# First-layer results of eight experts: transposed by way of DRAM and VectorE's block transposes instead of TensorE

## Chip, core and metric

The kernel runs on one NeuronCore of a Trainium2 chip. The metric is the device time of one execution in microseconds, as the median of several executions. The engines are TensorE (PE in the profile; its weight loads are PEld), VectorE (DVE), ScalarE (ACT), GpSimd (POOL) and SyncE (SP, which here only issues DMAs). Each works through its own instructions in order and waits on semaphores.

## What is computed

A graph layer over 625 nodes and 20,000 edges is followed by a mixture-of-experts layer over the 625 rows that come out (`x`, 625 x 1024, all in float32). Only the second matters here:

```python
sh = _gelu(jnp.einsum('td,sdh->sth', xf, sW1) + sb1[:, None, :])
shared = (jnp.einsum('sth,shd->std', sh, sW2) + sb2[:, None, :]).mean(axis=0)
gates = xf @ rW + rb
topk_vals, topk_idx = jax.lax.top_k(gates, TOP_K)           # two of eight
h = _gelu(jnp.einsum('td,edh->eth', xf, W1) + b1[:, None, :])
y = jnp.einsum('eth,ehd->etd', h, W2) + b2[:, None, :]
moe = jnp.einsum('te,etd->td', w, y)                         # w: softmax of the two
out = x + shared + moe
```

The model width is 1024, the hidden width 256 (`H`), and there are eight experts and two shared ones.

## The kernel before

The graph layer and the shared experts' first layer come first (to about 156 us). The rows that the router has given to the experts lie in 11 tiles of 128 slots (`NJ` = 11): tiles 4 to 10 are whole (one expert each), tiles 0 to 2 hold two experts of 64 slots, and tile 3 holds four of 32. A matmul of a part writes its own rows of the result, and parts run beside one another.

**First layer, loop at L1542.** The tiles are taken in the order 4, 5, 6, 0, 7, 1, 8, 2, 9, 10, 3 (`tiles`, L1533). In step `s` the code emits, in this order: the second half of the transposes of tile `s-1` (`turn`, L1490, only for tiles whose rows TensorE turns); the gather of tile `s` on GpSimd's queue and its transposition (`fetch`, L1474); the product with W1 of tile `s-1` (`expert_in`, L1508); and the middle of tile `s-2` (`expert_mid`, L1521).

- `fetch`: six tiles (`by_quarters`: 4, 5, 0, 1, 2, 10) are gathered as quarter rows by four indirect DMAs (L1465), so that VectorE's transposes of 32 x 32 blocks (L1482) give the columns that TensorE needs. The other five (6, 7, 8, 9, 3) are turned by TensorE in two halves (L1493, `p_x`); ScalarE copies the first half out of PSUM (L1499), VectorE the second (L1497). `copy_w1` (L1501) has ScalarE copy weights that a second or later part of a tile needs.
- `expert_in`: 16 matmul instructions for a whole tile into `p_h`, then VectorE copies `p_h` (128 slots x 256) to `hj` in SBUF (L1516, two buffers).
- `expert_mid`: TensorE turns the two 128 x 128 halves of `hj` into PSUM (L1524, `p_hT`), and ScalarE applies GELU with the bias and writes `hjT` (L1527), the stationary operand of the second layer.

The middles of the last two tiles (10 and 3) are emitted after the second-layer products of tile 4 (L1570).

**Second layer, loop at L1592.** The tiles are taken in the order 4, 5, 6, 0, 1, 2, 3, 7, 8, 9, 10 (`ORDER`). Each gives two halves of 512 columns (`expert_out`, L1559, `p_yj`); VectorE copies both halves to `ys` for the first four tiles, and later VectorE copies one and ScalarE the other (L1600, L1602); GpSimd scatters the rows to `yt` in DRAM (L1604). Ahead of it ScalarE makes 12 copies of W2 parts (`w2m`, L1590). Then SyncE loads `yt` back by node (L1615), while TensorE makes the shared experts' second layer (`p_o`, L1655, from `sw2` and `shT`), VectorE adds (L1626) and the rows are stored (L1640).

**What sets the order.** The engines' queues are laid out at compile time by a list scheduler that goes by the order of emission, its own estimate of when operands are ready, and the free buffers, so the order in the trace is near that of the code but not the same (the trace has some `p_o` products ahead of the second half of tile 6, for example). `tc.issue_after(x)` puts the instructions of its block behind `x` on their own engine, without a wait. PSUM has eight banks: five called `acc` (`p_x`, `p_yj`, most of `p_o`) and three called `mm` (`p_h`, `p_hT`, the rest of `p_o`).

**SyncE's queue** near the change: the eight 1 MB loads of `w2a` (L1179). The last, `load_w2(NE - 1)` at L1553, can start only when tile 5's product is done, because the turned rows of tiles 4 and 5 lie in that part of `w2a`. Then `sw2` (L1578, 2 MB), which takes memory that the first layer's weights held, and `x1` (L1581, 2.5 MB).

Of the kernel before, what the change touches and what calls it, by code (L numbers as in the profile page):

```python
# [8 lines left out]
F32 = mybir.dt.float32  # L9
# [5 lines left out]
AF = mybir.ActivationFunctionType  # L15
# [8 lines left out]
H = 256  # L24
NE = 8
NS = 2
TP = 125
# [16 lines left out]
NJ = 11  # L44
# [9 lines left out]
HK = H // 128  # L54
# [399 lines left out]
def sparse_kernel(  # L454
# [24 lines left out]
    nc = tc.nc  # L479

    def pool(stack, name, bufs=1, side="left", **kw):
        return stack.enter_context(tc.tile_pool(name=name, bufs=bufs, side=side,
                                                reuse_waits="tile", **kw))
# [5 lines left out]
    dram = ctx.enter_context(tc.tile_pool(name="dram", bufs=1, space=bass.MemoryType.DRAM))  # L489
    h2d = dram.tile([N, D], F32, name="h2d")  # L490
    x1d = dram.tile([N, D], F32, name="x1d")

    yt = dram.tile([2 * YB, D], F32, name="yt")

# [3 lines left out]
    def ps_mm(name):  # L498
        return psum[0].tile([128, 512], F32, tag="mm", name=name, bufs=3)
# [68 lines left out]
    ident = const.tile([128, 128], F32, name="ident")  # L568
# [210 lines left out]
    def first_row():  # L779
        x0 = xh[:TP, 0, :]  # L780
        h = rows.tile([TP, D], F32, tag="h", name="h_0")
        part = fbig.tile([TP, 3], F32, name="part")
        with tc.issue_after(behind.ins):
            nc.vector.tensor_reduce(part[:, 0:1], x0[:, :HALF], axis=AX.X, op=ALU.add)
        with tc.issue_after(table.ins):
            nc.scalar.activation(h[:, HALF:], x0[:, HALF:], AF.Identity, accum_out=part[:, 1:2])
        last = nc.vector.tensor_scalar(part[:, 2:3], part[:, 0:1], part[:, 1:2], -1.0 / D, op0=ALU.add, op1=ALU.mult)
        moved = nc.scalar.activation(h[:, :384], x0[:, :384], AF.Identity, bias=part[:, 2:3])
        with tc.issue_after(last.ins):
            last = nc.vector.tensor_scalar(h[:, 384:], x0[:, 384:], part[:, 2:3], None, op0=ALU.add)  # L790
        hs[0] = h
        return last, moved
# [264 lines left out]
    last, moved = first_row()  # L1057
# [120 lines left out]
    def load_w2(e):  # L1178
        nc.sync.dma_start(w2a[:, e], W2[e].rearrange("(k p) d -> p k d", p=128))  # L1179
# [261 lines left out]
    mid = pool(ctx, "mid")  # L1441
    hjT = mid.tile([128, NJ, HK, 128], F32, name="hjT")
    xts = ExitStack()
    xt = pool(xts, "xt", 2, side="right")
# [5 lines left out]
    def parts(j):  # L1450
        if j < NH2:
            return (0, HS, e_of[j]), (HS, 128, e_of[NH2 + j])
        if j < NM2:
            return [(QS * i, QS * (i + 1), e_of[nt + i]) for i in range(4)]
        return ((0, 128, e_of[NH2 + j - 1]),)

    xsT, p_hs, w1m = {}, {}, {}
    acts = []

    rows = {}  # L1460
# [1 line left out]
    def gather(j):  # L1462
        if j in by_quarters:
            for a in range(4):
                nc.gpsimd.indirect_dma_start(  # L1465
                    out=rows[j][:, a * (D // 4) : (a + 1) * (D // 4)], out_offset=None,
                    in_=h2d.rearrange("n (b f) -> (n b) f", b=4),
                    in_offset=bass.IndirectOffsetOnAxis(ap=tok4[:, a, j : j + 1], axis=0))
        else:
            nc.gpsimd.indirect_dma_start(  # L1470
                out=rows[j], out_offset=None, in_=h2d,
                in_offset=bass.IndirectOffsetOnAxis(ap=tok[:, j : j + 1], axis=0))

    def fetch(j):  # L1474
        if j in tiles[:2]:
            t_ = w2a[:, NE - 1, tiles.index(j)].rearrange("p (k n) -> p k n", k=KD)
        else:
            t_ = xt.tile([128, KD, 128], F32, tag="xsT", name=f"xsT_{j}")
        xsT[j] = t_
        if j in by_quarters:  # L1480
            with tc.issue_after(turned[-1].ins):
                nc.vector.transpose(t_.rearrange("p k (a r) -> p a k r", a=4), rows[j].rearrange("p (a c k) -> p a k c", a=4, k=KD))  # L1482
        else:
            half_row[j] = rows[j]
            turn(j, 0)
        copy_w1(j)
# [3 lines left out]
    def turn(j, g):  # L1490
        p = ps_acc(f"p_x{g}_{j}")
        for k in range(4):
            nc.tensor.transpose(p[:, k * 128 : (k + 1) * 128], half_row[j][:, 4 * g + k :: KD], ident)  # L1493
        o = xsT[j][:, 4 * g : 4 * g + 4, :]
        pv = p.rearrange("p (k n) -> p k n", k=4)
        if g:
            turned.append(nc.vector.tensor_copy(o, pv))  # L1497
        else:
            acts.append(nc.scalar.copy(o, pv))  # L1499
# [8 lines left out]
    def expert_in(j):  # L1508
        p = ps_mm(f"p_h_{j}")
        for k in range(KD):  # L1510
            for a, b, e in parts(j):
                nc.tensor.matmul(p[a:b, :H], xsT[j][:, k, a:b],  # L1512
                                 w1m[j, a][:, 0, k, :] if a else w1a[:, bass.ds(e, 1), k, :],
                                 start=(k == 0), stop=(k == KD - 1))
        h = xt.tile([128, H], F32, tag="hj", name=f"hj_{j}")
        nc.vector.tensor_copy(h, p[:, :H])  # L1516
        p_hs[j] = h

    bT = vT[:, KD + NS * HK :].rearrange("p (e t) -> p e t", t=HK)

    def expert_mid(j):  # L1521
        p = ps_mm(f"p_hT_{j}")
        for t in range(HK):
            nc.tensor.transpose(p[:, t * 128 : (t + 1) * 128], p_hs[j][:, t * 128 : (t + 1) * 128], ident)  # L1524
        for t in range(HK):
            for a, b, e in parts(j):
                done = nc.scalar.activation(hjT[:, j, t, a:b], p[:, t * 128 + a : t * 128 + b], AF.Gelu,  # L1527
                                     bias=bT[:, bass.ds(e, 1), t])
        acts.append(done)

# [2 lines left out]
    tiles = (*whole[:3], 0, whole[3], 1, whole[4], 2, *whole[5:], NH2)  # L1533
# [8 lines left out]
    for s in range(NJ + 2):  # L1542
        if 0 < s <= NJ and tiles[s - 1] in half_row:
            turn(tiles[s - 1], 1)
        if s < NJ:
            if s > 2:
                rows[tiles[s]] = io.tile([128, D], F32, tag="io", name=f"xs_{tiles[s]}")
                gather(tiles[s])
            fetch(tiles[s])
        if 0 <= s - 1 < NJ:  # L1550
            expert_in(tiles[s - 1])
        if s == 2:
            load_w2(NE - 1)  # L1553
        if 0 <= s - 2 < NJ - 2:
            expert_mid(tiles[s - 2])
    ORDER = (*whole[:3], *range(NM2), *whole[3:])
    w2m, p_ys = {}, {}

    def expert_out(j, s):  # L1559
        p_ys[j, s] = p = ps_acc(f"p_yj_{j}_{s}")  # L1560
        for k in range(HK):
            for a, b, e in parts(j):
                made = nc.tensor.matmul(p[a:b], hjT[:, j, k, a:b],  # L1563
                                        (w2m[j, a, k] if a else w2a[:, bass.ds(e, 1), k])[..., s * 512 : (s + 1) * 512],
                                        start=(k == 0), stop=(k == HK - 1))
        return made

    for s in range(2):
        expert_out(ORDER[0], s)
    for j in tiles[-2:]:  # L1570
        expert_mid(j)
    xts.close()
    in_w.close()

    late = pool(ctx, "late", side="right")
    sw2 = late.tile([128, NS, HK, D], F32, name="sw2")
    for i in range(NS):
        nc.sync.dma_start(sw2[:, i], sW2[i].rearrange("(k p) d -> p k d", p=128))  # L1578
    x1 = late.tile([TP, NT, D], F32, name="x1")
    for a, b in ((0, 3), (3, NT)):  # L1580
        nc.sync.dma_start(x1[:, a:b], x1d[a * TP : b * TP].rearrange("(t p) d -> p t d", p=TP))  # L1581
    gat = pool(ctx, "gat", 15, side="right")

    loads, (off,) = nc.values_load_multi_w_load_instructions(flag, min_val=0, max_val=EC * 4 + 1)
# [7 lines left out]
    for n, j in enumerate(ORDER):  # L1592
        y = gat.tile([128, D], F32, tag="y", name=f"ys_{j}")
        for s in range(2):
            at = slice(s * 512, (s + 1) * 512)
            if n:
                made = expert_out(j, s)
            p = p_ys[j, s]
            if s or n < 4:
                nc.vector.tensor_copy(y[:, at], p)  # L1600
            else:
                nc.scalar.copy(y[:, at], p)  # L1602

        sent.append(nc.gpsimd.indirect_dma_start(  # L1604
            out=yt, out_offset=bass.IndirectOffsetOnAxis(ap=row[:, j : j + 1], axis=0), in_=y, in_offset=None,
            bounds_check=2 * YB - 1, oob_is_err=False))
        for s in sent[:-1]:
            tc.declare_no_dep(sent[-1].ins, s.ins, reason="rows of different slots")

    gs = {}  # L1610
    for d in range(NT):
        for a in range(2):
            at = a * YB + 1 + d * TP
# [29 lines left out]
    for d in range(NT):  # L1643
# [3 lines left out]
        for at in ((0, 512), (512, D)) if d < NT - 1 else ((0, 512), (512, 768), (768, D)):  # L1647
            n = at[1] - at[0]
            at = slice(*at)
            p = (ps_mm if banks % 8 > 4 else ps_acc)(f"p_o_{d}_{at.start}")  # L1650
# [59 lines left out]
```

## Time and profile before

| What | us |
|---|---|
| Median of 3 runs (lowest, highest) | 285.66 (285.14, 286.66) |
| Profiled execution, time | 284.5 |
| Profiled execution, span of the trace | 282.6 |
| TensorE busy in the span | 276.2 (98%) |
| VectorE, ScalarE, GpSimd busy | 172.1, 100.4, 64.5 |
| First layer of the experts (first to last `p_h` product) | 156.5 to 202.1 |
| Second layer of the experts (`p_yj`) | 202.1 to 248.3 |
| Shared experts' second layer, from there to the last product | 248.3 to 277.6 |
| 22 transposes of `hj` (L1524), first and last start | 163.9, 205.9 |
| Granted TensorE clock | 1.00 |

The page lists, for each engine, busy time, share of the span and instructions; then the span in 40 slices; the DMA queues; the chain of work that ended last, by engine and line; and groups of instructions with busy time, mean duration in ns, and the idle time ahead of them with what ended it. A line of the timeline has the start and the duration in us, the engine (SPq is the issuing of DMAs on SyncE's queue), the line of the code, the operation, and output <- input. Matmuls overlap in the array, so the time that one takes from TensorE is the distance between starts, not its duration.

### The profile page before, as it was taken

The numbers are of one execution on the slowest core, as the hardware profiler recorded it, in microseconds if no ns is written. First come the engines' busy times: TensorE is split into PE (matmuls) and PEld (weight loads), VectorE is DVE, ScalarE is ACT, GpSimd is POOL, SyncE is SP. The second block draws the span as 40 slices with busy tenths as digits, with TensorE's granted clock in tenths as the row PEclk, the third lists the DMA queues.
The fourth block names the chain that finished last, engine by engine and source line by source line (L and its number), as shares of the span: only waits on it lengthen the run. The fifth ranks groups of instructions, "written<-read, shape, count | busy, mean of one in ns | idle before, by whom it ended". The sixth has DMA issues, their size and how long they took to land.

```text
span 282.6 us, 4458 instructions
## 1 busy us (share of the span) xinstructions
PE 276.2 (98%) x1531; PEld 185.1 (65%) x1531; DVE 172.1 (61%) x435; ACT 100.4 (36%) x232; POOL 64.5 (23%) x128
## 2 busy tenths in 40 slices
PE   8999999999999999999999999999999999999992
PEld 6777777788888555677777887778544324444452
DVE  5899999999875889838911444323330211116892
ACT  3456418334642323354101363564089011100000
POOL 9810110000000023411046655540020222210000
PEclk9999999999999999999999999999999999999999
DMA  7999981000000999995999484440284453339982
GB/s 238 362 334 359 345 288 48 2 0 2 1 0 9 389 371 425 424 415 195 387 410 394 134 271 129 125 147 4 57 335 181 181 216 139 148 135 349 380 306 78
DMA packets 22084, 61.58 MB, mean 218 GB/s; under 512 B 2467, under 2 KB 8294, under 8 KB 21033
## 3 DMA queue, kind: packets, MB, share of 16 engines
q1 hardware_dynamic: 16093, 44.32, 42.3%
q0 software_dynamic: 5680, 16.58, 16.3%
q10 hardware_dynamic: 284, 0.35, 0.4%
q8 instruction: 14, 0.23, 0.4%
q14 instruction: 13, 0.11, 0.1%
HBM read 43.19 MB, written 18.82 MB: 219 GB/s over the span
## 4 chain that ended last, share of the span: by engine, by line
PE 88%; DVE 6%; DMA 3%; SPq 1%; ACT 0%; issue 0%
PE p_pr L955 15%; PE p_h L1512 14%; PE p_yj L1563 14%; PE p_o L1655 12%; PE p_sh L1145 12%; PE p_y L1030 6%; PE p_agg L984 5%; DMA xh<-in_x_dram 3%; DVE st L776 2%; PE cnt L933 2%; PE p_x L1493 2%; PE p_t L843 2%; DVE ohs L902 1%; PE p_hT L1524 1%; PE p_gate L1195 1%; PE p_y L1031 1%
## 5 line engine op out<-in xcount | busy, mean ns | idle before, releaser
L955 PE MATMUL p_pr<-wg,nT 128*125 128x286 f32 x240 | 62.2, 409 | 0.2
L955 PEld LDWEIGHTS p_pr<-wg,nT 128*125 128x125 f32 x240 | 43.3, 187 | 12.5 <-ACT nT L849 1.2
L1563 PE MATMUL p_yj<-w2a,hjT 128*128 (+2 forms) x88 | 38.8, 595 | 0.0
L1655 PE MATMUL p_o<-sw,shT 128*125 128x512 f32 (+1 forms) x88 | 36.1, 553 | 0.0
L1145 PE MATMUL p_sh<-h2T,sw 128*128 128x313 f32 (+1 forms) x128 | 35.3, 429 | 0.0
L1512 PE MATMUL p_h<-w1a,xsT 128*128 (+2 forms) x144 | 32.7, 380 | 0.0
L1600 DVE COPY ys<-p_yj 128x512 f32<-128x512 f32 x15 | 10.4, 691 | 36.0 <-PE p_yj L1563 36.0
L1563 PEld LDWEIGHTS p_yj<-w2a,hjT 128*128 128x128 f32 (+2 forms) x88 | 14.4, 168 | 22.7 <-issue 22.1
L1145 PEld LDWEIGHTS p_sh<-h2T,sw 128*128 128x128 f32 x128 | 23.6, 189 | 8.5 <-issue 0.2
L1655 PEld LDWEIGHTS p_o<-sw,shT 128*125 128x125 f32 x88 | 16.4, 187 | 17.1 <-issue 16.1
L1512 PEld LDWEIGHTS p_h<-w1a,xsT 128*128 128x128 f32 (+2 forms) x144 | 22.8, 163 | 6.5
L1465 POOL DMA_INDIRECT xs<-h2d,tok x24 | 22.7, 946 | 18.5 <-PE p_x L1493 7.6
L1604 POOL DMA_INDIRECT yt<-ys,row x11 | 10.7, 970 | 52.1 <-DVE ys L1600 52.1
L1041 POOL DMA_DIRECT2D x1d<-xh x10 | 5.7, 576 | 71.7 <-DVE flagf L726 62.1
L1516 DVE COPY hj<-p_h 128x256 f32<-128x256 f32 x11 | 4.7, 425 | 25.4 <-PE p_h L1512 25.4
L1030 PE MATMUL p_y<-wo_t,eT 128*125 128x512 f32 (+1 forms) x40 | 18.8, 592 | 0.0
L1527 ACT ACTIVATE hjT<-p_hT,vT 128x128 f32<-128x128 f32 (+2 forms) x34 | 8.6, 335 | 23.9 <-PE p_hT L1524 23.9
L984 PE MATMUL p_agg<-P,CT 125*125 125x288 f32 x100 | 15.5, 305 | 0.0
L1512 PE MATMUL p_h<-w1m,xsT 128*64 128x256 f32 (+1 forms) x96 | 14.7, 381 | 0.0
L1563 PE MATMUL p_yj<-w2m,hjT 128*64 128x512 f32 (+1 forms) x48 | 14.1, 595 | 0.0
L1626 DVE SCALAR_TENSOR_TENSOR x<-g,wab,x 125x1024 f32<-125x1024 f32 (+1 forms) x12 | 13.2, 1105 | 1.4 <-DMA g<-yt 1.2
L903 DVE TENSOR_TENSOR ohs<-ohs,cols 125x1024 f16<-125x1024 f16 (+1 forms) x22 | 14.0, 636 | 0.0
(307 smaller groups left out, 417.6 us busy)
## 6 DMA issues: line engine op xcount, KB each, us to landing
w1a<-in_L_ffn_W_dram SPq DMA_DIRECT2D x8, 1024.0 KB
w2a<-in_L_ffn_W_dram SPq DMA_DIRECT2D x8, 1024.0 KB
yt<-zero SPq DMA_DIRECT2D x2, 2560.0 KB
g<-yt SPq DMA_DIRECT2D x10, 512.0 KB
sw<-in_L_ffn_sW_dram SPq DMA_DIRECT2D x4, 1024.0 KB
x1d<-xh POOLq DMA_DIRECT2D x5, 448.0 KB
h2d<-h POOLq DMA_DIRECT2D x5, 448.0 KB
out_dram<-x SPq DMA_DIRECT2D x4, 448.0 KB
```

What stands on the lines that cost most here:

```text
L903: last = nc.vector.tensor_tensor(os, os, both(VV_, 128)[1], op=ALU.mult)
L955: product = nc.tensor.matmul(p[:TP, :F], nT[:, k, m * TP : (m + 1) * TP], wg[:, k, r, :], start=(k == 0), stop=(k == KD - 1))
L984: nc.tensor.matmul(p[:TP, : F + 2], CT[:, m, at : at + TP], P[:, m, r, i], start=(m == 0 and i == 0), stop=(m == NT - 1 and i == 1))
L1030: nc.tensor.matmul(ps[s][:TP, :], eT[:n, k, :], wo_t[:n, k, at], start=(k == 0), stop=False)
L1145: nc.tensor.matmul(p[:, : z - a], sw1[:, i, k, t * 128 : (t + 1) * 128], h2T[:, k, a:z], start=(k == 0), stop=(k == KD - 1))
L1465: nc.gpsimd.indirect_dma_start(out=rows[j][:, a * (D // 4) : (a + 1) * (D // 4)], out_offset=None, in_=h2d.rearrange("n (b f) -> (n b) f", ...
L1512: nc.tensor.matmul(p[a:b, :H], xsT[j][:, k, a:b], w1m[j, a][:, 0, k, :] if a else w1a[:, bass.ds(e, 1), k, :], start=(k == 0), stop=(k == ...
L1563: made = nc.tensor.matmul(p[a:b], hjT[:, j, k, a:b], (w2m[j, a, k] if a else w2a[:, bass.ds(e, 1), k])[..., s * 512 : (s + 1) * 512], star ...
L1600: nc.vector.tensor_copy(y[:, at], p)
L1604: sent.append(nc.gpsimd.indirect_dma_start(out=yt, out_offset=bass.IndirectOffsetOnAxis(ap=row[:, j : j + 1], axis=0), in_=y, in_offset=No ...
L1626: added.append(nc.vector.scalar_tensor_tensor(*args, op0=ALU.mult, op1=ALU.add))
L1655: nc.tensor.matmul(p[:TP, :n], shT[:, i, k, own], sw2[:, i, k, at], start=(i == 0 and k == 0), stop=False)
```

## The change

The two TensorE transposes of each tile's `hj` go. Instead:

- VectorE's copy writes `hj` with the columns in another order (quarters of 64: for each, 32 of the first 128 columns and 32 of the second), into one buffer instead of two. SyncE stores `hj` to a new DRAM tensor `hd` and then loads it back in four DMAs, one for each group of 32 partitions of `hjT`, so that partition group `q` holds quarter `q` of the columns of all 128 slots.
- VectorE's block transpose of 128 x 256 turns that to `hT`, a new SBUF tile with one buffer, and GELU reads `hT` (SBUF) where it read `p_hT` (PSUM).
- The middle of a tile is emitted one step later (`s-3`), behind the `hj` copy of that step. The last two move into the second-layer loop, behind the copies of its second and third tile.
- `sw2` is issued after the last store of `hj`, the last tile's four loads after `sw2`, and `x1` after `sw2` too.

```diff
+    hd = dram.tile([NJ, 128, H], F32, name="hd")
...
-        h = xt.tile([128, H], F32, tag="hj", name=f"hj_{j}")
-        nc.vector.tensor_copy(h, p[:, :H])
-        p_hs[j] = h
+        h = xt.tile([128, H], F32, tag="hj", bufs=1, name=f"hj_{j}")
+        copied.append(nc.vector.tensor_copy(h.rearrange("p (q c r) -> p c q r", q=4, c=HK),
+                                           p[:, :H].rearrange("p (c q r) -> p c q r", c=HK, q=4)))
+        moved.append(nc.sync.dma_start(hd[j], h))
+        if j != tiles[-1]:
+            to_quarters(j)
+
+    def to_quarters(j):
+        for q in range(4):
+            nc.sync.dma_start(hjT[32 * q : 32 * q + 32, j].rearrange("t c (b r) -> t (c b r)", b=4)
+                              .rearrange("t (b x) -> t b x", b=4),
+                              hd[j].rearrange("(b t) (q x) -> q t b x", b=4, q=4)[q])
...
     def expert_mid(j):
-        p = ps_mm(f"p_hT_{j}")
-        for t in range(HK):
-            nc.tensor.transpose(p[:, t * 128 : (t + 1) * 128], p_hs[j][:, t * 128 : (t + 1) * 128], ident)
+        p = mid.tile([128, HK, 128], F32, tag="hT", name=f"hT_{j}")
+        with tc.issue_after(copied[-1].ins):
+            nc.vector.transpose(p.rearrange("p c (b t) -> p c b t", b=4),
+                                hjT[:, j].rearrange("p c (b r) -> p (c b r)", b=4)
+                                .rearrange("p (b c r) -> p c b r", b=4, c=HK))
...
-                done = nc.scalar.activation(hjT[:, j, t, a:b], p[:, t * 128 + a : t * 128 + b], AF.Gelu,
+                done = nc.scalar.activation(hjT[:, j, t, a:b], p[:, t, a:b], AF.Gelu,
...
-        if 0 <= s - 2 < NJ - 2:
-            expert_mid(tiles[s - 2])
+        if 0 <= s - 3 < NJ - 2:
+            expert_mid(tiles[s - 3])
...
-    for j in tiles[-2:]:
-        expert_mid(j)
...
     for i in range(NS):
-        nc.sync.dma_start(sw2[:, i], sW2[i].rearrange("(k p) d -> p k d", p=128))
+        with tc.issue_after(moved[-1].ins):
+            last = nc.sync.dma_start(sw2[:, i], sW2[i].rearrange("(k p) d -> p k d", p=128))
+    with tc.issue_after(last.ins):
+        to_quarters(tiles[-1])
...
     for a, b in ((0, 3), (3, NT)):
-        nc.sync.dma_start(x1[:, a:b], x1d[a * TP : b * TP].rearrange("(t p) d -> p t d", p=TP))
+        with tc.issue_after(last.ins):
+            nc.sync.dma_start(x1[:, a:b], x1d[a * TP : b * TP].rearrange("(t p) d -> p t d", p=TP))
...
-                nc.vector.tensor_copy(y[:, at], p)
+                copied.append(nc.vector.tensor_copy(y[:, at], p))
...
+        if n in (1, 2):
+            expert_mid(tiles[n - 3])
```

More of the change, by code (lines that the diff above doesn't have):

```diff
@@ L1455, in parts @@
         return ((0, 128, e_of[NH2 + j - 1]),)
-    xsT, p_hs, w1m = {}, {}, {}
+    xsT, w1m, copied, moved = {}, {}, [], []
     acts = []
```

## The prediction, made before the changed kernel was run

> **What bounds the kernel now.** I read the page first: engine shares, then the chain.
>
> ```profile
> PE 276.2 (98%) x1531; PEld 185.1 (65%) x1531; DVE 172.1 (61%) x435; ACT 100.4 (36%) x232; POOL 64.5 (23%) x128
> ...
> PE 88%; DVE 6%; DMA 3%; SPq 1%; ACT 0%; issue 0%
> ...
> L1516 DVE COPY hj<-p_h 128x256 f32<-128x256 f32 x11 | 4.7, 425 | 25.4 <-PE p_h L1512 25.4
> ```
>
> TensorE is busy from end to end, and from the start of the experts (156.5 us) to the last product (277.6) the chain is TensorE alone; VectorE waits for it (25.4 us ahead of the `hj` copies). So time taken off TensorE there is time off the kernel, unless it becomes a wait. Next the timeline at one step of the experts' loop (start, duration, engine):
>
> ```profile
> 184.86 0.36 PEld L1524 LDWEIGHTS p_hT<-ident,hj 128*128 128x128 f32 x2
> 185.08 0.38 PE L1524 MATMUL p_hT<-ident,hj 128*128 128x128 f32 x2
> 185.19 0.52 PEld L1493 LDWEIGHTS p_x<-ident,xs 128*128 128x128 f32 x4
> 185.28 0.42 DVE L1516 COPY hj<-p_h 128x256 f32<-128x256 f32 x1 [0.76 <-PE p_h L1512]
> 185.30 0.49 PE L1493 MATMUL p_x<-ident,xs 128*128 128x128 f32 x3
> ```
>
> Read starts, not durations: the two transposes of `hj` start at 185.08, the next work at 185.30. A pair holds TensorE for 0.22 us. Last, the line of the block transposes, and SyncE's queue (start, time of the issues):
>
> ```profile
> L1482 DVE STREAM_TRANSPOSE xsT<-xs x4: 2031/2046/2056, 165.4 to 191.0; 128x1024 f32<-128x1024 f32 x4
> ```
>
> ```profile
> 0.75 0.39 SPq L531 DMA_DIRECT2D ety_i<-in_edge_type_dram  x1
> 1.20 0.41 SPq L531 DMA_DIRECT2D src_i<-in_src_dram  x1
> 1.65 0.43 SPq L546 DMA_DIRECT2D xh<-in_x_dram  x1
> ```
>
> ```profile
> 132.82 31.64 SPq L1179 DMA_DIRECT2D w2a<-in_L_ffn_W_dram  x8
> 202.19 0.88 SPq L1578 DMA_DIRECT2D sw<-in_L_ffn_sW_dram  x2
> 203.12 4.69 SPq L1581 DMA_DIRECT2D x<-x1d  x2
> ```
>
> SyncE can start a DMA every 0.45 us, and between 164.5 and 202.2 it has nothing to do. The change puts a chain of its own there.
>
> **Removed.** 22 transposes, 11 pairs. Six pairs in the loop cost 0.22; three that follow a half tile cost 0.28 (172.37 to 172.65); the last two together 0.44 (205.61 to 206.05). Sum 1.32 + 0.84 + 0.44 = **2.6 us**, all on the bounding engine. Nothing on TensorE waited for `hj`, so no stall goes with it; the bounds are 2.4 (all at 0.22) and 2.9 (the short gaps after half tiles close too). [...]
>
> **Added on VectorE and ScalarE.** One block transpose of 128x256 for each tile: a quarter of L1482's 2.04 us, so 0.51 (bounds: 0.42, the copy of as many elements, and 2.04). In the fullest step VectorE has the copy 0.43, the transpose 0.51, the copy of `p_x` 0.69 and L1482 2.04, together 3.67 of a step of 4.0: it fits. Behind the new transpose stands the copy of `p_x` (172.49 + 0.43 + 0.51 + 0.69 = 174.12); the product needs it after its first eight matmuls, 173.09 - 0.28 + 1.7 = 174.5. Spare: 0.4 us. That is the thinnest cover in the loop: a late transpose stalls TensorE almost one for one. GELU out of SBUF and the permuted order of the `hj` copy I take at their old price (within 0.1 us either way); TensorE waits for neither inside the loop, since products of the second layer begin after it.
>
> **Added on SyncE and in the queues.** For each tile one store of 128 KB (1 KB rows) and four loads of 32 KB in 256 B pieces. No row shows this pair. The nearest by the trace's records of DMA completions: the output store of 112 rows of 1 KB issued at 277.02 has landed on most of its 16 engines after 1.8 us, on the last after 3.8; that of 117 rows at 278.08 after 1.7 and 2.5; the 78 KB load issued at 0.75 after 1.9, the next after 3.0. I take 1.85 for the store (1.7 to 3.8) and 1.9 for a load (1.6 to 3.0), the typical engine, since the loop moves 43 to 313 GB/s and stragglers are few there. Round trip: 0.1 + 1.85 + 0.1 + three starts of 0.45 + 1.9 = 5.3 us. The block transpose comes two steps after the copy, 8.0 us: hidden, with 2.7 to spare. SyncE, in order, is held by a tile for 0.1 + 1.85 + four starts (1.8) = **3.75 us, of a step of 4.0** (202.24 - 160.20 over ten steps is 4.2, less 0.2). It just keeps up. With one `hj` buffer, the copy of the next tile also waits for the store.
>
> One transfer breaks into this: the last `w2a` load, 1 MB, issued at 164.09 and landed 5.2 us later, in the window 164.5 to 168.7 with a DMA share of 0.89 at 313 GB/s. In the changed kernel SyncE ends tile 4's loads at 160.7 + 1.85 + 0.1 + 1.8 = 164.45, and `w2a` is ready before tile 5's copy ends (164.55): it goes first, and tile 5's store lands behind it in the same rings at 164.45 + 5.2 + 0.2 = 169.85. Its four loads hold SyncE till 171.75, tile 6's store lands at 173.65, and only then may VectorE copy tile 0 (due at 172.05): copy 174.13, transpose 174.64, `p_x` 175.33. TensorE needs `p_x` at 173.09 - 0.72 + 1.7 = 174.07. **Stall 1.3 us**, once; later steps catch up by 0.25 each. Bounds: 0 (the store goes first) and 2.
>
> **Moved.** Tiles 10 and 3 get transpose and GELU after the second and third second-layer tile. ScalarE's twelve `w2m` copies (11.5 us) then start near 202 instead of 207.9 and end near 214, the two GELU groups (2.04 us) near 216; tile 3's products begin at 230.8. Tile 3's four loads queue behind the 2 MB of `sw2` and land near 214; behind its transpose VectorE has the copies of the next second-layer tiles, which are at 220.4 and later now, after one at 211.4. Cost 0; were TensorE to take those tiles first, VectorE would hold them 1 to 2 us, with five PSUM banks to cover it. `sw2` is issued after the last store, 0.6 to 2.4 us later than now; it landed at 212.2, and `p_o`, which TensorE pulls forward to 211.2, needs the second half of it at 212.9. Taken at 0; bound 2.1 if the order stays and SyncE lags. `x1` is wanted at 252 and landed by 236.5: hidden. The 3 MB of traffic meets the gathers, which are issued a step or more ahead: hidden.
>
> **Sum.** The profiled execution took 284.5 (span 282.6 and 1.9 around it): -2.6 + 1.3 = -1.3 gives 283.2. It lies 1.2 under the median of the runs, so the forecast for the median is 285.66 - 1.3 = **284.4**.
>
> **Rivals.** *Everything hidden*: the store of tile 5 goes ahead of `w2a`, or the copy of `p_x` ahead of the transpose; 285.66 - 2.6 = **283.1**. For it: 0 us of idle TensorE now and 2.7 us of spare in the round trip. Against: `w2a` is ready first.
>
> *SyncE's chain sets the step* (the slower side). The place is the one `hj` buffer: the copy of the last tile, due at 200.1, waits for the ninth store after the jam, 169.85 + 8 S, with S SyncE's time per tile. At S = 3.75 that is 199.85, in time. If the store's last engine takes 2.5 us as at 278.08, S = 4.45, 205.45, 5.3 late: -2.6 + 5.3 gives **288.4**. It costs more than the gain from S = 4.1 (a store of 2.2 us) and is measurably slower from 4.3; at a store of 3.8 it would be over 295, against which speaks that the others of the same DMA were done at 1.8. [...] The records above show 1.7 to 1.8 for most engines.
>
> *Late second half*: `sw2` or the last loads stall TensorE behind the loop on top of the jam, 1 to 2 us: about **285.9**. That the change leaves transposes of `hj` on TensorE is excluded by its text; those of `xs` stay.
>
> **How the numbers follow.** 0.5% is 1.43 us, about what a measurement of this kernel can tell from no change: faster is under 284.2, slower over 287.1. The forecast 284.4 (283.8 to 285.2) has 0.32, of which 0.13 below 284.2; everything hidden 0.25; SyncE's chain 0.35 (286.3 to 292), of which 0.33 above 287.1; late second half 0.08, 0.03 of it above. Faster 0.38, same 0.26, slower 0.36. Cutting a tenth on each side, the range is 282.8 to 289.5; the forecast's own is 283.8 to 285.2. Two signs are open because the gain is fixed and small and the cover on SyncE is 0.25 us a tile.
>
> **What would show it.** Right: no `p_hT` on TensorE, one gap of about 1.3 us before the first `p_h` with `p_x` after 172, SyncE issuing five DMAs per tile within 4 us, the block transposes at 0.5. Wrong: `hj` copies waiting for a DMA step after step (SyncE's chain), block transposes waiting for loads (round trip over 8 us), idle TensorE ahead of `p_o` at 211 (late `sw2`), or a block transpose well over 0.9 us, at which the 0.4 us of spare is gone in every step with `p_x`.

## The result, and the profile after

The changed kernel takes 293.94 us (median of 6 runs, 291.97 to 298.25) beside 285.88 us (6 runs) of the kernel before: ratio 1.0297, 95% interval 1.026 to 1.0334. It is slower by 8 us, where 284.4 was forecast and 289.5 was the end of the range. The profiled execution took 295.12 us, its span is 293.3 (before 284.5 and 282.6): the traces differ by 10.7 us, more than the medians, because the profiled execution lies above the median here and below it before.

From the page of the changed kernel, the lines that answer to those of before:

```profile
PE 280.2 (96%) x1509; PEld 184.2 (63%) x1509; DVE 175.4 (60%) x446; ACT 101.7 (35%) x232; POOL 64.6 (22%) x128
...
PEclk9999999999999999999999999999955999999999
...
PE 78%; DMA 9%; DVE 7%; issue 2%; POOL 1%; SPq 1%; ACT 1%; DVEq 0%; ACTq 0%
...
L1672 PE MATMUL p_o<-sw,shT 128*125 128x512 f32 (+1 forms) x88 | 41.2, 612 | 5.9 <-DMA sw<-in_L_ffn_sW_dram 5.9
```

22 TensorE instructions are gone (1531 to 1509), yet TensorE is busy 4 us longer. `p_o` has the 88 products of before, at a mean of 612 ns instead of 553, and 5.9 us of idle time that waits for `sw2`; its line before was:

```profile
L1655 PE MATMUL p_o<-sw,shT 128*125 128x512 f32 (+1 forms) x88 | 36.1, 553 | 0.0
```

The row of the granted clock shows two slices at 5, between 213 and 227 us. The chain is no longer TensorE alone: 9% is DMA.

The groups of the two VectorE instructions of the change, and TensorE at a step of the loop:

```profile
L1534 DVE STREAM_TRANSPOSE hT<-hjT 128x256 f32<-128x256 f32 x11 | 4.8, 434 | 0.0
L1517 DVE COPY hj<-p_h 128x256 f32<-128x256 f32 x11 | 4.5, 413 | 15.4 <-DMA hd<-hj 11.0 <-PE p_h L1513 3.6 <-DVE xsT L1483 0.8
```

```profile
175.75 1.89 PE L1513 MATMUL p_h<-w1a,xsT 128*128 x8
177.47 0.60 PE L1494 MATMUL p_x<-ident,xs 128*128 128x128 f32 x4
178.01 0.43 PE L1513 MATMUL p_h<-w1a,xsT 128*64 x1
```

A block transpose takes 0.43 us. The `hj` copies, which used to wait for TensorE only (25.4 us), wait 11.0 us for the store of the tile ahead. On TensorE nothing stands between product and `p_x` any more, and it waits for nothing of the change in the loop: the products of tile 5 start 1.46 us later than before (0.40 of it is there at the first product of tile 4; the rest comes with a wait of 0.91 us for rows whose gather landed late), those of tile 10 start 0.06 us earlier. The first second-layer products end at 211.38 us, before at 211.37. Then comes the loss. TensorE from there:

```profile
215.25 3.75 PE L1672 MATMUL p_o<-sw,shT 128*125 128x512 f32 x4 [3.86 <-DMA sw<-in_L_ffn_sW_dram]
221.05 3.78 PE L1672 MATMUL p_o<-sw,shT 128*125 128x512 f32 x4 [2.06 <-DMA sw<-in_L_ffn_sW_dram]
224.62 0.63 PE L1674 MATMUL p_o<-b,wT 96*125 96x512 bf16 x1
225.04 3.79 PE L1672 MATMUL p_o<-sw,shT 128*125 128x512 f32 x6
228.67 0.59 PE L1575 MATMUL p_yj<-w2a,hjT 128*128 x1
```

Windows of the same stretch: bounds, length, TensorE's busy time (instructions), granted clock, DMA share, GB/s:

```profile
211.00:216.00 5.00, 1.14 (x2) 0.75 0.93 318
216.00:221.00 5.00, 2.99 (x4) 0.50 0.91 348
221.00:226.00 5.00, 4.95 (x7) 0.50 0.33 132
```

Before, two halves of `p_o` (a half is eight products and one for the bias) were pulled forward here and ran at clock 1.00, 3.65 us each:

```profile
211.20 3.60 PE L1655 MATMUL p_o<-sw,shT 128*125 128x512 f32 x8
214.85 3.60 PE L1655 MATMUL p_o<-sw,shT 128*125 128x512 f32 x8
218.51 2.45 PE L1563 MATMUL p_yj<-w2a,hjT 128*128 x5
```

Now TensorE, at the same point of its work, is back at the second layer at 228.67. Of these 17.5 us it waits for 5.9. In the other 11.5 it makes one half and six products of the next, for which the rows of before, at clock 1.00, give an estimate of 6.2: the granted clock is 0.50 from 213.5 us, within the first wait, to 227.2, and that costs 5.3 us. The rest of the second half (two products and the bias) runs at the end, from 276.6 to 277.7. Together 11.2 us are lost, and TensorE's last product ends 11.2 us later than before (288.83 against 277.59).

`sw2` was late because of its place in SyncE's queue. SyncE's issues near the end of the loop (start, time of the issues; before, `sw2` stood at 202.19):

```profile
199.61 1.73 SPq L1525 DMA_DIRECT2D hjT<-hd  x4
201.43 0.39 SPq L1519 DMA_DIRECT2D hd<-hj  x1
203.21 1.74 SPq L1525 DMA_DIRECT2D hjT<-hd  x4
205.05 0.38 SPq L1519 DMA_DIRECT2D hd<-hj  x1
206.83 1.73 SPq L1525 DMA_DIRECT2D hjT<-hd  x4
208.65 0.38 SPq L1519 DMA_DIRECT2D hd<-hj  x1
209.14 0.95 SPq L1589 DMA_DIRECT2D sw<-in_L_ffn_sW_dram  x2
```

From four loads to the next four: 3.6 us a tile, near the 3.75 of the prediction. But `sw2` leaves 7.0 us later than before: tile 3's product ends 2.2 us later (the scheduler has put four products of tile 4 among tile 3's), its copy waits 2.6 for the store ahead, its store 1.7 behind that tile's loads, `sw2` 0.5 behind the store. It also lands more slowly, 6.0 and 11.4 us after issue instead of 4.8 and 9.6, beside two scatters of `yt` that are issued at 209.17 and 210.68.

### The profile page after: what moved, and what is told of

It is laid out like the page before. It is cut to its first block, busy times and chain, and to the rows that moved or that the text cites. A ratio compares the mean times of both kernels' runs of the same rounds, so it can differ in the third digit from the quotient of the medians.

```text
span 293.3 us, 4560 instructions
## 1 busy us (share of the span) xinstructions
PE 280.2 (96%) x1509; PEld 184.2 (63%) x1509; DVE 175.4 (60%) x446; ACT 101.7 (35%) x232; POOL 64.6 (22%) x128
## 4 chain that ended last, share of the span: by engine, by line
PE 78%; DMA 9%; DVE 7%; issue 2%; POOL 1%; SPq 1%; ACT 1%; DVEq 0%; ACTq 0%
PE p_pr L956 15%; PE p_h L1513 12%; PE p_o L1672 12%; PE p_yj L1575 12%; PE p_sh L1146 7%; PE p_y L1031 6%; PE p_agg L985 5%; DMA sw<-in_L_ffn_sW_dram 4%; DMA xh<-in_x_dram 3%; DMA xs<-h2d,tok 2%; DVE st L777 2%; PE cnt L934 2%; PE p_x L1494 2%; PE p_t L844 1%; DVE w2a L1483 1%
## 5 line engine op out<-in xcount | busy, mean ns | idle before, releaser
L1672 PE MATMUL p_o<-sw,shT 128*125 128x512 f32 (+1 forms) x88 | 41.2, 612 | 5.9 <-DMA sw<-in_L_ffn_sW_dram 5.9
L1672 PEld LDWEIGHTS p_o<-sw,shT 128*125 128x125 f32 x88 | 17.8, 206 | 26.3 <-issue 21.6
L1621 POOL DMA_INDIRECT yt<-ys,row x11 | 10.7, 970 | 61.7 <-DVE ys L1614 61.7
L1539 ACT ACTIVATE hjT<-hT,vT 128x128 f32<-128x128 f32 (+2 forms) x34 | 9.8, 354 | 30.3 <-DVE hT L1534 23.0
L1513 PE MATMUL p_h<-w1m,xsT 128*64 128x256 f32 (+1 forms) x96 | 15.3, 382 | 0.0
L985 PEld LDWEIGHTS p_agg<-P,CT 125*125 125x125 f32 x100 | 13.7, 186 | 0.2
```

Of the source, the lines that this page charges most:

```text
L985: nc.tensor.matmul(p[:TP, : F + 2], CT[:, m, at : at + TP], P[:, m, r, i], start=(m == 0 and i == 0), stop=(m == NT - 1 and i == 1))
L1513: nc.tensor.matmul(p[a:b, :H], xsT[j][:, k, a:b], w1m[j, a][:, 0, k, :] if a else w1a[:, bass.ds(e, 1), k, :], start=(k == 0), stop=(k == ...
L1621: sent.append(nc.gpsimd.indirect_dma_start(out=yt, out_offset=bass.IndirectOffsetOnAxis(ap=row[:, j : j + 1], axis=0), in_=y, in_offset=No ...
L1672: nc.tensor.matmul(p[:TP, :n], shT[:, i, k, own], sw2[:, i, k, at], start=(i == 0 and k == 0), stop=False)
```

## Experiments

All ratios are to the kernel before on the same chip.

| Kernel | What is changed | Median us | Ratio, 95% interval |
|---|---|---|---|
| e1_sw2_pool | changed kernel, `sw2` on GpSimd's queue | 287.47 | 1.007 (1.0042 to 1.0097) |
| e2_po_behind | changed kernel, no `p_o` pulled forward | 287.4 | 1.0048 (1.0016 to 1.008) |
| e3_no_trip | changed kernel without store and loads | 282.99 | 0.9908 (0.9874 to 0.9942) |
| e4_w2_pool | changed kernel, last `w2a` load on GpSimd's queue | 293.23 | 1.032 (1.0241 to 1.0398) |
| b2_late_sw2 | kernel before, `sw2` delayed | 294.52 | 1.032 (1.028 to 1.0359) |
| e11_pool_two | e1 with the two halves of `p_o` of before | 283.89 | 0.9939 (0.9911 to 0.9968) |
| e9_pool_behind | e1 and e2 together | 287.62 | 1.0051 (1.001 to 1.0092) |
| e6_store_act | changed kernel, stores on ScalarE's queue | 285.53 | 1.0004 (0.9973 to 1.0035) |
| e13_no_gather | changed kernel without eight gathers | 293.36 | 1.0288 (1.0246 to 1.0329) |
| e14_late_w2 | changed kernel, last `w2a` load later in the code | 292.66 (one run) | none |
| e15_pool_two_late_w2 | e11 with the same | 283.76 | 0.9947 (0.992 to 0.9974) |
| e16_order | changed kernel, orders of before on VectorE and TensorE | 288.35 | 1.009 (1.0053 to 1.0126) |
| e17_order_pool_two | e11 and e16 together | 288.91 | 1.0105 (1.0048 to 1.0163) |
| e18_order_no_gather | e13 and e16 together | 283.94 | 0.9966 (0.9933 to 0.9998) |

### What the loss is

**Without the trip.**

```diff
-        h = xt.tile([128, H], F32, tag="hj", bufs=1, name=f"hj_{j}")
-        copied.append(nc.vector.tensor_copy(h.rearrange(...), ...))
-        moved.append(nc.sync.dma_start(hd[j], h))
-        if j != tiles[-1]:
-            to_quarters(j)
+        copied.append(nc.vector.tensor_copy(hjT[:, j].rearrange(...), ...))
```

> The change without its trip through memory: VectorE's copy of hj goes straight to the tile that the quarter loads would fill, so the store and the four quarter loads of each tile are gone, with SyncE's chain; the block transposes stay. This leaves out the exchange of quarters between partitions: the output is not the reference's. sw2 is issued when its space is free. All theories that put the loss behind SyncE (A, B, C): 282.5 to 284 us, the 2.6 us of the removed transposes below before (less the wait on a late gather). A theory that puts the loss in VectorE's block transposes or in GELU out of SBUF: 287 us or more.

Ratio 0.9908: 0.0092 x 285.43 = 2.6 us gained (1.7 to 3.6 by the interval). The transposes were worth what the prediction said, and block transposes and GELU out of SBUF cost nothing that shows. All the loss lies in the trip and what hangs on it.

**`sw2` away from SyncE.**

```diff
-        with tc.issue_after(moved[-1].ins):
-            last = nc.sync.dma_start(sw2[:, i], ...)
+        nc.gpsimd.dma_start(sw2[:, i], ...)
```

> The two loads of sw2 (2 MB) are issued on GpSimd's queue instead of SyncE's and wait for no store; SyncE's chain of store and quarter loads, the one hj buffer and all its traffic stay, and tile 3's quarter loads now go straight behind its store. Theory A (the loss is sw2, issued 7 us late behind the lagging chain, with p_o pulled forward onto it and the clock halved after the wait): TensorE's idle time ahead of p_o goes, the ten us lost there come back: 283 to 285.5 us, ratio to before 0.99 to 1.0. Theory B (SyncE's chain itself: VectorE and ScalarE late through the one hj buffer): only the part that lies on sw2 goes, the products of tiles 10 and 3 become late instead; 290 us or more. Theory C (the traffic of small pieces slows the other transfers): sw2 still lands late though it is issued early; 291 to 293 us.

6.5 us come back (293.94 against 287.47), less than theory A has. `sw2` is issued at 202.91, TensorE waits 0.4 us for it, the clock is 1.00 in every window to 270 us. Theories B and C fall. What is missing stands at the end of the kernel, TensorE's last product and VectorE's last adds:

```profile
276.47 0.27 PE L1673 MATMUL p_o<-b,wT 96*125 96x256 bf16 x1
277.12 0.69 DVE L1642 SCALAR_TENSOR_TENSOR x<-p_o,x 125x512 f32<-125x512 f32 x1
277.73 1.53 DVE L1642 SCALAR_TENSOR_TENSOR x<-g,wab,x 125x512 f32<-125x512 f32 x2
...
279.37 0.76 DVE L1642 SCALAR_TENSOR_TENSOR x<-p_o,x 125x256 f32<-125x256 f32 x2
```

TensorE is through at 276.74, 0.85 us earlier than before (277.59), but VectorE ends 3.4 us behind it, at 280.13: here the scheduler pulled three halves of `p_o` forward instead of two, so the second layer, the rows of `yt` and the adds came later.

**The same with two halves**, fixed by hand as in the kernel before:

```diff
+            if n == 2 and s:
+                for d, o in ((2, slice(512, D)), (3, slice(0, 512))):
+                    p = pulled[d, o.start] = ps_mm(f"p_o_{d}_{o.start}")
+                    with tc.issue_after(made.ins):
+                        made = product(d, o, p)
```

> As e1_sw2_pool (sw2 on GpSimd's queue), with exactly the two halves of p_o pulled forward that the kernel before pulls, where e1 pulled three: those put the second layer 3.65 us later, the rows of yt and the adds of VectorE with it, and the adds ended the kernel. If that is what was left of the loss in e1 (287.5 against 283.0 without the trip): 283.5 to 285 us. If what is left is the lag of hj on VectorE and ScalarE: 286 to 288 us as before it.

283.89: faster than the kernel before by 0.0061 x 285.73 = 1.7 us. From the changed kernel it differs in `sw2`'s queue (and so the place of tile 3's loads) and in the second half of `p_o`, of which the changed kernel pulls forward six products and this one all; the difference is 10 us (293.9 against 283.9). The `hj` copies lag in this kernel too (tile 8's at 193.80, 7 us behind its product), and it costs at most the 0.9 us to e3. This is the best version that computes all.

**The delay alone, in the kernel before.**

```diff
+    trip = sw2[:, 0, 0, :H]
+    hold = nc.sync.dma_start(trip, sW2[0, :128, :H])
+    for i in range(3):
+        with tc.issue_after(hold.ins):
+            hold = nc.sync.dma_start(*((trip, hd) if i % 2 else (hd, trip)))
```

> The kernel before, with TensorE's transposes and its own order of products (two halves of p_o pulled forward, fixed by hand), and sw2 alone delayed: four small DMAs, each waiting for the one ahead, stand before it on SyncE, about 4 x 1.75 = 7 us. No trip of hj, no change else. Theory A (sw2 late times p_o pulled forward is most of the loss): TensorE waits for sw2 in the two places of the changed kernel, about 4 + 2 to 4 us, the clock falls after the wait, and the time is 292 to 297 us. Theory B (the loss is in the chain of hj, and sw2 only looks like it): 286 to 289 us.

The four trips put `sw2` at 211.60, 9.4 us late, and the loss is there with every transpose on TensorE:

```profile
219.00 5.20 PE L1606 MATMUL p_o<-sw,shT 128*125 128x512 f32 x8 [7.19 <-DMA sw<-in_L_ffn_sW_dram]
224.04 0.38 PE L1608 MATMUL p_o<-b,wT 96*125 96x512 bf16 x1
224.26 3.60 PE L1606 MATMUL p_o<-sw,shT 128*125 128x512 f32 x8
```

A wait of 7.19, then eight products in 5.0 us that take 3.4 at full clock (the next eight do); the granted clock is 0.50 from 216 to 221 us. Theory A holds: with e11 it is shown from both sides.

**No `p_o` pulled forward**, with `sw2` late (e2) and on GpSimd's queue (e9):

```diff
-            with tc.issue_after((made if d < 2 else loads[mybir.EngineType.PE]).ins):
+            with tc.issue_after(made.ins):
```

> sw2 stays as late as in the changed kernel; only TensorE's order is changed: every p_o stands behind the last product of the second layer, none is pulled forward. Theory A (sw2 late times p_o pulled forward): nothing waits for sw2, which has landed by 221 where p_o then begins near 235: 283 to 285.5 us, a wait of at most 1 us ahead of p_o. Theory B (the chain is late for the second layer itself: the blocks of tiles 10 and 3): with no p_o to fill in, TensorE waits for GELU's results of the last tiles instead and 288 to 294 us remain. Theory C (traffic): as B, spread over many waits.

> sw2 on GpSimd's queue and every p_o behind the second layer: e1 and e2 together. TensorE then waits neither for sw2 nor, through VectorE's queue, for tile 3's quarter loads behind the 2 MB of sw2 (2.1 us in e2's profile). What is left is the lag of SyncE's chain in the loop (p_h waited 2.1 us for the copy of p_x in e2's profile). If the three costs are separate: 283.5 to 286 us. If p_o is needed as filler while GELU's results of the last tiles are missing: 287 us or more.

Both near 287.5, with runs from 284.6 to 292.7: the wait for `sw2` is gone, another takes its place. Of e2 VectorE, then TensorE (its profiled execution is one of the longer ones, 290.25, so the waits may be longer than usual):

```profile
224.82 0.45 DVE L1534 STREAM_TRANSPOSE hT<-hjT 128x256 f32<-128x256 f32 x1 [9.02 <-DMA hjT<-hd]
225.19 1.85 DVE L1614 COPY ys<-p_yj 128x512 f32<-128x512 f32 x3
```

```profile
225.90 0.64 PE L1575 MATMUL p_yj<-w2a,hjT 128*64 x1 [2.09 <-DVE ys L1614]
```

VectorE stands 9.0 us in tile 3's transpose, whose quarter loads are issued at 211.93, behind the 2 MB of `sw2` (210.61); three `ys` copies stand behind it, and TensorE, which has no `p_o` to go on with, waits for their PSUM banks. In e9 the loads are in time (a wait of 0.7 us), but the transpose waits 8.1 us for ScalarE's GELU, and TensorE 2.7 for `ys`. Where `p_o` is pulled forward (e11) TensorE has neither wait, so it does serve as cover.

### Why `sw2` was late

**The last `w2a` load.** e4 issues it on GpSimd's queue; e14 and e15 (on top of e11) move it from `s == 2` to `s == 9` in the code.

```diff
-            load_w2(NE - 1)
+            nc.gpsimd.dma_start(w2a[:, NE - 1], ...)
```

> As the changed kernel, but the last w2a load (1 MB) is issued on GpSimd's queue, so that it is not in SyncE's queue beside tile 5's store. Theory A1 (the lag of SyncE comes from that load in its queue; after it the chain runs at 3.6 us a tile in steps of 4.2): the lag at the loop's end falls from 7 us to 1 to 4 us, sw2 is issued at 203 to 206 instead of 209 and the time falls to 284.5 to 290 us. Theory A2 (the load fills all the rings wherever it is issued): the stores and loads of tiles 5 and 6 are as late as before, sw2 within 1 us of 209, and 292 to 295 us.

> The changed kernel with the last w2a load (1 MB) moved seven tiles back in SyncE's order, behind the gathers. Theory G: the hj copies of tiles 0 to 2 lag by 3 us or more all the same. Theory W: they lag by under 1.5 us. The time is not the question, since the load now stands shortly before sw2: 290 to 297 us by either.

> e11_pool_two (sw2 on GpSimd's queue, the order of before for p_o) with the last w2a load moved back as in e14, to see whether the 0.9 us between e11 and the kernel without the trip (283.9 against 283.0) goes with it. Theory W: 283.0 to 283.6 us. Theory G, or a collision of the load with sw2: 283.9 us or more, up to 287 where p_o waits for sw2 again.

e4: `sw2` is issued at 207.57, in a run whose loop began 0.9 us earlier; 293.2 us; theory A2. With the load on GpSimd's queue the store behind it is no quicker: issued at 168.65, it landed after 5.1 us, in the changed kernel after 5.0 (issued at 170.82). e14 and e15 tell nothing of the load: the scheduler issued it at 165.46 and 164.78 all the same, so e15 is a second e11, and repeats it (283.76).

**The gathers.** In e13 the eight later tiles take earlier rows (`rows[tiles[s]] = rows[...]` for the gather).

> The changed kernel without the gathers of tiles 0 to 3 and 7 to 10 in the loop (the eight tiles behind the first three take the rows of an earlier tile, so the output is not the reference's); stores, quarter loads, the last w2a load and sw2 behind the last store all stay. Theory G (SyncE's chain falls behind because the gathers keep the queues full, where its store lands after 3.5 to 5 us instead of 1.7): the hj copies lag behind p_h by at most 1 us after the w2a load, sw2 is issued at 204.5 to 206.5 and the time is 285 to 289 us. Theory W (the w2a load alone starts the lag, and a tile's 3.6 to 3.75 us recover it too slowly in steps of 4.1): lag and time about as in the changed kernel, 291 us or more.

DMA share in 170 to 190 falls from 0.84 and 0.64 to 0.24 and 0.23, stores land after 1.7 to 1.9 us (3.0 for the one beside the `w2a` load), and nothing changes: 293.4 us, `sw2` at 208.11. Theory G misses; theory W has the time, but not the reason. VectorE says why:

```profile
189.49 0.69 DVE L1498 COPY xsT<-p_x 128x512 f32<-128x512 f32 x1 [4.85 <-PE p_x L1494]
190.10 2.03 DVE L1483 STREAM_TRANSPOSE xsT<-xs 128x1024 f32<-128x1024 f32 x1
192.05 0.38 DVE L1517 COPY hj<-p_h 128x256 f32<-128x256 f32 x1
```

The copy at 192.05 is tile 8's, whose product ended at 184.8. VectorE stood idle for 4.85 us in front of a `p_x` that belongs to tile 9: the order laid out at compile time has that copy and a block transpose of 2.03 us ahead. In the kernel before, tile 8's `hj` copy comes ahead of them:

```profile
185.28 0.42 DVE L1516 COPY hj<-p_h 128x256 f32<-128x256 f32 x1 [0.76 <-PE p_h L1512]
190.41 0.69 DVE L1497 COPY xsT<-p_x 128x512 f32<-128x512 f32 x1 [0.43 <-PE p_x L1493]
```

The changed kernel has the order of e13 and nearly its time:

```profile
190.51 0.69 DVE L1498 COPY xsT<-p_x 128x512 f32<-128x512 f32 x1 [3.46 <-PE p_x L1494]
193.07 0.39 DVE L1517 COPY hj<-p_h 128x256 f32<-128x256 f32 x1
```

From there SyncE's 3.6 us a tile make up only 0.5 of each 4.1. Why the scheduler chose this order no run shows. One `hj` buffer alone does not bring it about: e6, below, has one too, and the order of before.

**VectorE's order of the kernel before**, in the changed kernel (e16), with e11 (e17), and without gathers (e18):

```diff
+            with tc.issue_after(copied[-1].ins):
                 turned.append(nc.vector.tensor_copy(o, pv))
...
-        expert_out(ORDER[0], s)
+        with tc.issue_after(put[-1].ins):      # put: last product of each p_h
+            expert_out(ORDER[0], s)
```

> The changed kernel with VectorE's order of the kernel before: the copy of p_x (and the block transpose of xs behind it) stands behind the hj copy of the tile ahead, where the changed kernel has it in front of the hj copies of tiles 0, 1, 8 and 9; TensorE's first products p_yj stand behind the last p_h, as in the kernel before. sw2 stays behind the last store. Theory V (the lag comes from that order: in the changed kernel, and without its gathers too, the hj copy of tile 8 stands behind a copy of p_x that has its operand only at 190 us; SyncE's 3.6 us a tile then make up 0.5 a tile only): the hj copies follow p_h within 1.5 us from tile 1 on, sw2 is issued at 203 to 206, TensorE stalls once by 0.5 to 2.5 us ahead of a p_h behind the w2a load, and the time is 284 to 288 us. Theory S (SyncE's chain under load is too slow by itself): the lag stays at 3 us or more and, now in front of the copies of p_x, stalls TensorE tile after tile: 290 us or more.

> e11_pool_two (sw2 on GpSimd's queue, two halves of p_o pulled forward) with VectorE's order of the kernel before, as in e16. Theory V: the quarter loads are in time, sw2 is in time, only the stall of 0.5 to 2.5 us ahead of a p_h is left: 283.3 to 286 us. Theory S: 287 us or more, since the lag that e11 hides behind TensorE then stalls it.

> e16_order (VectorE's order of the kernel before) without the gathers of the eight later tiles, as in e13 (those tiles take earlier rows, so the output is not the reference's). In e16 the stores of tiles 6 and 7, issued at 169.33 and 180.02, landed after 4.5 and 4.7 us under the gathers, and the hj copies of tiles 0 and 1 waited 5.1 and 5.9 us for them. Theory G+V (both are needed for the lag: the gathers' load on the queues, or else the order that the changed kernel has instead): a store lands after 1.7 us behind the w2a load, a tile takes SyncE 3.6 us, the hj copies follow p_h within 1 us from tile 7 on, sw2 is issued at 202.5 to 205 and the time is 283 to 286 us. Theory S (the chain is too slow even on empty queues): stalls of 2 us or more behind tile 7 remain and 287 us or more.

e16 gives neither theory whole: 288.35, but the lag is back, now by the DMAs. Its VectorE:

```profile
184.81 0.42 DVE L1519 COPY hj<-p_h 128x256 f32<-128x256 f32 x1 [5.89 <-DMA hd<-hj]
185.48 0.45 DVE L1536 STREAM_TRANSPOSE hT<-hjT 128x256 f32<-128x256 f32 x1 [0.24 <-DVE hj L1519]
185.85 0.65 DVE L1499 COPY xsT<-p_x 128x512 f32<-128x512 f32 x1
```

The store ahead, issued at 180.02, landed after 4.7 us beside the gathers; the copy of `p_x` is now behind that wait, and TensorE loses 3.1 us to it (1.5 the longest) and 0.9 to gathers. `sw2` is late as well (208.58) but so is TensorE, and `p_o` waits for nothing. e17 is the same with `sw2` issued at 208.80, when its space is free (TensorE waits 3.1 us for VectorE, 1.3 for a gather): theory S. Then e18, the same order on empty queues, SyncE:

```profile
199.39 0.38 SPq L1521 DMA_DIRECT2D hd<-hj  x1
201.16 1.73 SPq L1527 DMA_DIRECT2D hjT<-hd  x4
202.99 0.38 SPq L1521 DMA_DIRECT2D hd<-hj  x1
203.47 0.95 SPq L1591 DMA_DIRECT2D sw<-in_L_ffn_sW_dram  x2
```

283.94 us. Behind the `w2a` load, from the store issued at 173.72 on, a tile's loads leave 1.7 to 1.8 us after its store (2.8 and 3.3 in two cases of seven), the `hj` copies wait for TensorE again (17.9 us in nine waits, for a store 5.4 in two), `sw2` leaves at 203.47, and TensorE waits for nothing in the loop. So two causes cover for one another: VectorE's order in the changed kernel, and, where that is mended, the stores beside the gathers. Take away both and SyncE keeps up, `w2a` load and all; take away one and it does not. Two things stay open: e16 and e18 set TensorE's order too (tile 4's products behind tile 3's), which no run separates from VectorE's, and e18 gains 1.0 us on the kernel before where e3 gains 2.6.

**The stores on ScalarE's queue.**

```diff
-        moved.append(nc.sync.dma_start(hd[j], h))
+        moved.append(nc.scalar.dma_start(hd[j], h))
```

> The stores of hj go on ScalarE's queue, so that no store stands behind the four loads of the tile ahead; the loads stay on SyncE, sw2 is issued when its space is free. Theory L1 (the lag is SyncE's order: a tile holds the queue for store landing plus four starts, 3.6 us unloaded and 5 to 6 while gathers run): the lag of the hj copies behind p_h falls under 2 us at every tile, sw2 is issued near 202.5 and the time is 283 to 285.5 us. Theory L2 (the lag is the one hj buffer and the landing of the stores under load alone): the copies lag by 3 us or more in the steps with gathers, and 286 us or more.

285.53, no gain and no loss: `sw2` leaves at 205.40 and nothing waits for it, but the `hj` copies still wait for stores (9.2 us in two waits, 5.7 the longest), and TensorE 3.8 us for VectorE. The time lies between the two theories. The copies on VectorE stand in the order of before here, so the run differs from the changed kernel in more than the stores' queue and does not separate the theories; it shows that with one `hj` buffer waits for stores under load remain. Two `hj` buffers were not tried.

## Why the prediction was wrong, point by point

- **Removed, 2.6 us: right.** e3 measures 2.6 (1.7 to 3.6).
- **Added on VectorE and ScalarE: right.** 0.43 us for a block transpose (0.51 forecast, 0.42 the lower bound), 354 ns for a GELU instead of 335, neither on TensorE's path.
- **SyncE's time per tile: right for empty queues, wrong under load.** 3.6 us where the trace shows it undisturbed (3.75 forecast). The prediction took the engine that is typical and held that "stragglers are few there". In e18 the loads left 1.7 to 1.8 us after most stores, but 3.3 us after the one issued at 194.30 (at 197.56). Beside gathers and the `w2a` load it is more than a straggler: of the changed kernel's store issued at 170.82 the first of the five recorded completions came after 3.4 us, the last after 4.98, and only then, at 175.81, did the loads leave. The change adds 256 KB of its own a tile.
- **The jam, 1.3 us once: not there as told.** It supposed that the `w2a` load goes ahead of tile 5's store, but the store left first (166.46, the load at 166.93). And it supposed VectorE's order of before, with the copy of `p_x` behind the waiting `hj` copy. In the changed kernel the two had changed places: no stall, and in its stead an `hj` copy up to 7 us late. With the order that was supposed (e16) TensorE does stall, by 3.1 us in three waits, and without gathers (e18) not at all, `w2a` load or not.
- **Moved: the step that failed.** "`sw2` is issued after the last store, 0.6 to 2.4 us later than now [...] Taken at 0; bound 2.1 if the order stays and SyncE lags." It was issued 7.0 us later and cost 11.2 in the trace. The place, the wait and its condition were named, among what would show the prediction wrong too ("idle TensorE ahead of `p_o` at 211"). Three sizes failed: the lag was taken from an order on VectorE that the changed kernel does not have; the landing was left as before; and a wait was priced at its length, when the halved clock cost 5.3 us on top of 5.9. The bound should have followed the lag: the rival just below allowed the last `hj` copy to start at 205.45, 5.3 us late (it started at 206.93), and `sw2` stands behind the store of that copy.
- **Rivals.** *SyncE's chain sets the step* had the sign, and the lag nearly to size, but put the price of that lag (5.3 us, 288.4) on the loop without naming the wait of TensorE; in the changed kernel TensorE waits for nothing of it in the loop. That e16, where the lag does stall TensorE in the loop, gives 288.35 is luck: it loses 3.1 us to VectorE and 0.9 to gathers, not 5.3. *Late second half* had the place at 1 to 2 us and a chance of 0.08. That 7 us of lag and `sw2` belong to one case was not seen.
- **Tile 3's loads and x1: hidden, as forecast**, in the changed kernel. The loads are done on their first engine at 219.7, on the last at 222.2, instead of near 214, covered by TensorE's own lateness; where `p_o` does not cover them (e2) they cost 2.1 us.
- **Open:** at 211.4 TensorE should have been 1.1 us ahead of before by the later start (1.5) and the gain (2.6), and was level. Some of it goes where products of tile 4 stand among tile 3's; the rest was not traced.

## What to carry to other kernels

When a change puts a chain of small DMAs on a queue, follow the queue to its end: what hurt here is the large load that has to leave behind the last of them, at a place far from the change, and the lag that it inherited is that of the whole chain (`sw2`, 7.0 us late, 11.2 us lost). An order laid out at compile time is part of the change: instructions that seemed untouched can change places, and a cover worked out from the old order then says nothing. Price a wait of TensorE with the clock that the trace shows behind it (here 5.9 us of waiting, and 5.3 more at a clock of 0.50).

## What the runs showed of the hardware

- **TensorE's granted clock fell to 0.50 within a wait of 3.9 us.** It is 0.50 from 216 to 226 us behind the wait of 3.86, through a second one of 2.06, and 0.88 in the five microseconds after; it had fallen 2.1 us into the first wait (1.00 from 211.4 to 213.5, 0.50 from 213.5 to 215.2). Behind the wait of 7.19 in b2 eight products took 5.0 us instead of 3.4. In e2 a wait of 2.15 us at 185.8 left the clock at 1.00 and one of 2.09 at 225.9 was followed by 0.66 from 225 to 230. From what length of wait on the clock falls, these runs do not show. The clock was not in the prediction's sum.
- **The small DMAs are quick alone.** In the changed kernel, from 197.8 to 208 us, a store of 128 rows of 1 KB had landed, by its last recorded completion, after 1.7 to 1.8 us, 32 KB in 256 B pieces after 1.6 to 1.9, with starts 0.35 to 0.48 us apart; the same store took 3.0 us beside the `w2a` load (e13, e18), 4.7 beside gathers (e16, issued at 180.02), and 5.0 beside both (changed kernel, issued at 170.82).
